# A transformer block on one core: the heads' sums loaded and inverted later, the feed-forward part started earlier

## The chip, the core and the metric

The kernel runs on one NeuronCore of a Trainium2 chip. Five instruction streams matter: TensorE (PE in the profile: matmuls and transposes), VectorE (DVE), ScalarE (ACT), GpSimd (POOL) and SyncE (SP, which issues nearly all DMAs). The metric is the device time of one launch in microseconds (us). Before the change the median of three runs is 856.14 us, with 854.97 the least and 856.69 the most.

## The reference

The input x has 4 sequences of 512 rows with 512 features. All is float32.

```python
x = x + attn(layernorm(x))
x = x + ffn(layernorm(x))

def attn(h):                                     # 32 heads of 16
    q, k, v = split(h @ w_attn + b_attn)
    s = q @ k.T / 16 + slope[head] * (key - row)  # ALiBi, causal
    return (softmax(s) @ v).reshape(...) @ w_proj + b_proj

def ffn(h):                                      # inner size 1376
    return (silu(h @ w_gate.T) * (h @ w_up.T)) @ w_down.T
```

layernorm has no weights; its eps is 1e-5.

## The kernel before, in words

**Slots.** The kernel writes its program through a heap of events. `at(t, fn, args)` puts a step at time t, in "slots"; `spread` lays a list of steps evenly between two times, `gemms` does that for matmul steps, and `later(dt, fn)` puts a step dt slots after the one that calls it. At the end the events are taken in order of time and each issues its instructions. A slot is no fixed time on the chip: the slots set the order only. In this kernel a slot of the attention phase is a little over one microsecond. PE keeps exactly this order, and so does SP's DMA queue (line 77, `Ordered`). Instructions that are wrapped in `pin` keep it too, among pinned ones of the same engine. The rest of DVE, ACT and POOL is ordered by a scheduler in the compiler.

**Precision.** Matmuls with weights are made of three products: each factor is split into a rounded high part (ACT, line 241 for weights) and a low part (DVE, line 242), and high*high, high*low and low*high are summed in a PSUM bank of 128x512 (eight banks in all).

**Attention.** There are 32 sub-units `su` of four heads, eight for each of the four sequences (b = 0 to 3), each 10 slots long. `pass_a` computes the scores from a stack of q and k (`st`), and DVE reads off their maxima (line 542: tile `bank` masked with `mask_t`, result read into M). A bank is free for the next scores only when DVE is through with it. `to_row` turns the maxima into rows of the stack (L571, and a DMA on POOL's queue). `pass_b` computes the scores again, ACT takes the exponential (L594, tile P), POOL masks the diagonal blocks (L596), and PE multiplies by v (bank<-P,v; starts at slot 10 su + 8.6). ACT copies the sums to `ue` (L616), and SP writes them to DRAM as `ud`. The stacks of a later sub-unit come back from DRAM by six DMAs `st<-qd` of 128 KB each. Where a tile is numbered, `st` has four buffers in turn.

**The heads' ends.** A unit u is two sub-units, eight heads; row 16 of each head's block in `ud` is the sum of its exponentials. The path is:

- `head_sums(u)`: SP loads the sums, lc<-ud, 16 KB. This can't start before both halves of `ud` have been written.
- `inverses(u)`: DVE takes the reciprocal, rc<-lc (line 641, pinned), and some slots later SP writes rd<-rc.
- `attn_heads(u)`: SP loads uc<-ud (256 KB) and rb<-rd, the inverse repeated over 16 rows (256 KB).
- `scaled_heads(u)`: POOL multiplies uc by rb (L662, pinned, so ahead of what the scheduler puts later on POOL), ACT (L665) and DVE (L666) split the product into `aT`.
- `proj_steps(b, t)`: matmuls of aT with w_proj; the input rows `xr` are loaded, POOL adds the bias (L434), DVE adds the bank (L438), and SP writes x1d<-xr to DRAM.

The projections of sequences 0, 1 and 2 are laid between the matmuls of the attention as filler for PE.

**Feed-forward.** `norm_steps` (from line 111) loads four tiles xt<-x1d, takes the statistics on DVE (L127, pinned, and L128), the root on POOL (L132, L134) and applies them on DVE (L144). `transposed` turns the tiles on PE (L88), and ACT and DVE split them into xnT. `ffn(b, times)` lays out, for each of eleven blocks of the inner size, the gate and up products (bank<-xnT,wf), ACT's Silu (L865), the product and its split (DVE L869 and L872, ACT L871), and the down product. `weights(t, kind, ...)` issues two loads (raw<-in_wgu or raw<-in_wd, 256 KB each) at slot t and their splits into `wf` six slots later. There are 17 such loads for the first sequence, and the weights then stay for the others.

**Buffers.** The tiles xt, raw, ue, uc, rb, xr and sg share nine buffers (tag "x"), in the order of their allocation; xnT, aT and hl share ten. SP has eight semaphore lanes, used in turn: a DMA on SP also waits until the one before it on its lane has landed.

The lines that the change touches: 47 (`ffn`), 647 (the delay of rd's write), 754 to 756 (times of `head_sums` and `inverses`), 757 to 761 (heads and projections of sequences 0 to 2), 765 (the projection of the last sequence), 831 to 834 (the weights' times) and 842 to 851 (the norm in `ffn`).

Of the kernel before, what the change touches and what calls it, by code (L numbers as in the profile page):

```python
# [24 lines left out]
NT = S // 128  # L25
NK = HID // 128
KM = 59
FAR = -30000.0
PRM = {
    'lv': 1,  # L30
    'lf': 0,
    'lg': 0,
    'P1': 4,
    'sv': [1, 2],
    'tn': 6,
    'vc': 1,
    'q3': 0.865,
# [6 lines left out]
    'pin': '',  # L44
    'wp': 84.0,
    'order': 's',
    'ffn': 311.954,
    'ffs': 8.623,
    'pj3': 346.0,
    'nb': 10.709,  # L50
# [10 lines left out]
def f(ap):  # L61
    return ap.bitcast(F32)
# [3 lines left out]
def block_kernel(ctx, tc, x, wqk, wv, bqk, bv, wp, bp, wgu, wgul, wd, cst, out):  # L66
    nc = tc.nc
    def pin(ins):
        return tc.keep_in_program_order(ins)
# [14 lines left out]
    def matmul(*args, **kw):  # L84
        tc.keep_in_program_order(nc.tensor.matmul(*args, **kw))  # L85
# [10 lines left out]
    def bank():  # L96
        return ps.tile([128, 512], F32, tag="bank", bufs=8, name="bank")
# [131 lines left out]
    def xnT_tiles(pl):  # L229
        return [pl.tile([128, 2, S], FR, tag="t4", bufs=PRM["t4"], name="xnT") for _ in range(NK)]  # L230
# [95 lines left out]
    def at(t, fn, *args):  # L326
        heapq.heappush(events, (max(t, clock["now"]), clock["n"], fn, args))
        clock["n"] += 1

    def later(dt, fn, *args):  # L330

        at(clock["now"] + dt, fn, *args)

    def spread(t0, t1, steps):
        for n, (fn, *args) in enumerate(steps):
            at(t0 + (n + 0.5) * (t1 - t0) / len(steps), fn, *args)

    def mm3_steps(get_p, pairs, done):

        todo = [(a, c) for (w, x2) in pairs for a, c in ((w(0), x2(0)), (w(0), x2(1)), (w(1), x2(0)))]  # L340
        box = {}

        def one(n):
            if n == 0:
                box["p"] = get_p()
            a, c = todo[n]
            matmul(box["p"], a(), c(), start=(n == 0), stop=(n == len(todo) - 1))
            if n == len(todo) - 1:
                done(box["p"])

        return [(one, n) for n in range(len(todo))]
# [64 lines left out]
    def proj_steps(b, t):  # L416
        c = slice(t * 128, t * 128 + 128)

        def w(k):
            return lambda h: (lambda: aTs[4 * b + k][:, h, c])  # L420

        def xx(k):
            return lambda h: (lambda: Wp[k // 2][:, h, k % 2, :])

        r0 = b * S + t * 128
        box = {}

        def start():
            box["xr"] = com.tile([128, HID], F32, tag="x", bufs=PRM["xb"], name="xr")
            sp.dma_start(box["xr"], x[r0 : r0 + 128, :])  # L430
            return bank()

        def add_bias():
            pin(pool.tensor_tensor(box["xr"], box["xr"], bp_t, ALU.add))  # L434

        def done(p):
            xr = box["xr"]
            dve.tensor_tensor(xr, p, xr, ALU.add)  # L438

            def send():  # L440
                sp.dma_start(x1d[r0 : r0 + 128, :], xr)
                made.add(("x1", b, t))

            later(4.5, send)

        steps = mm3_steps(start, [(w(k), xx(k)) for k in range(4)], done)
        return steps[:10] + [(add_bias,)] + steps[10:]
# [191 lines left out]
    def inverses(u):  # L639
        rc = com.tile([128, 32], F32, tag="rc", bufs=2, name="rc")  # L640
        pin(dve.reciprocal(rc, lcs[u]))

        def send():
            rds[u] = dr.tile([8, S], F32, tag="rd", bufs=16, name="rd")
            sp.dma_start(rds[u].rearrange("h (a q) -> (h a) q", a=16), rc)

        later(4.5 if u < 15 else 2.5, send)

    def attn_heads(u):

# [22 lines left out]
    def gemms(t0, t1, *items):  # L673
        spread(10.0 * t0, 10.0 * t1, [s for item in items for s in item])
# [50 lines left out]
    for su in range(NS):  # L725
        t0 = 10.0 * su
        t = t0 - 20.6
# [7 lines left out]
    for b in range(B):  # L735
        t = 8 * b
# [3 lines left out]
        if b + 1 < B:  # L740
            xT_next(b + 1, 10.0 * (t + PRM["xt"]) if b else 7.6)
            u = 4 * b + 4
# [9 lines left out]
                    t + 6.2, t + 8.2, qk_steps(u + 2, 0), qk_steps(u + 2, 1), v_steps(b + 1, 0), v_steps(b + 1, 1),  # L752
                )
    for u in range(4 * B):
        at(20.0 * u + 28.5, head_sums, u)
        at(20.0 * u + 33.0, inverses, u)
    for b, first, gap, p0, p1_ in ((0, 102.0, 5.0, 127.0, 148.0), (1, 182.0, 5.0, 207.0, 228.0), (2, 246.0, 6.0, 274.0, 298.0)):
        for k in range(4):
            at(first + gap * k, attn_heads, 4 * b + k)
            at(first + 8.0 + gap * k, scaled_heads, 4 * b + k)  # L760
        gemms(p0 / 10, p1_ / 10, *[proj_steps(b, t) for t in range(NT)])
    for u, t in ((12, 313.0), (13, 316.0), (14, 320.5), (15, 340.0)):
        at(t, attn_heads, u)
        at(t + 6.0, scaled_heads, u)
    gemms(PRM["pj3"] / 10, PRM["pj3"] / 10 + 4, *[proj_steps(3, t) for t in range(NT)])


    GU, DN = {}, {}
# [46 lines left out]
    def weights(t, kind, it, slot, wait=6.0):  # L815
        loads, rest = (gu_steps if kind == "gu" else dn_steps)(it, slot)
        for n, ((l, a), (r, c)) in enumerate(zip(loads, rest)):
            at(t + 0.5 * n * bool(wait), l, a)
            at(t + 0.5 * n * bool(wait) + wait, r, c)
# [5 lines left out]
    loads = []  # L825
# [2 lines left out]
        if it % 2 == 0:  # L828
            loads.append(("dn", it, len(loads)))

    for n, t in enumerate((297.0, 311.0, 305.0, 314.0, 328.0, 322.0)):
        weights(t, *loads[n])
    at(PRM["tl"], open_late)
    for n, t in enumerate((331.0, 345.0, 339.0, 348.0, 362.0, 356.0, 366.0, 379.0, 373.0, PRM["pj3"] + 36.0, PRM["pj3"] + 44.0)):
        weights(t, *loads[6 + n])

    def ffn(b, times):

        box = {}
        xs = []  # L840
        t0 = times[0]
        loads, rest = norm_steps(x1d, b, xs, (1,))
        spread(t0 - (23.0 if b else 24.0), t0 - (18.0 if b else 20.0), loads)
        spread(t0 - (15.5 if b else 18.0), t0 - (8.0 if b else 10.0), rest)

        def tp(k):
            if k == 0:
                box["xT"] = xnT_tiles(com)
            transposed(xs, box["xT"], [k])

        spread(t0 - 8.5, t0, [(tp, k) for k in range(NK)])

        def up_gate(it, t):
            m = min(128, INTER - it * 128)
            at_once = {}

            def w(g, k):
                return lambda h: (lambda: GU[it][:, h, g, k])

            def x2(k):  # L860
                return lambda h: (lambda: box["xT"][k][:, h, :])

            def gate(p):
                at_once["sg"] = sg = com.tile([128, S], F32, tag="x", bufs=PRM["xb"], name="sg")
                act.activation(sg[:m], p, AF.Silu)  # L865

            def up(p):
                sg = at_once["sg"]
                dve.tensor_tensor(sg[:m], sg[:m], p, ALU.mult)  # L869
                hl = com.tile([128, 2, S], FR, tag="t4", bufs=PRM["t4"], name="hl")  # L870
                act.copy(hl[:m, 0, :], sg[:m])  # L871
                dve.tensor_tensor(hl[:m, 1, :], sg[:m], f(hl[:m, 0, :]), ALU.subtract)  # L872
                box[it] = hl

            steps = []
            for g, done in enumerate((gate, up)):
                steps += mm3_steps(lambda: bank()[:m], [(w(g, k), x2(k)) for k in range(NK)], done)
            spread(t, t + PRM["ffs"] * 2 / 3, steps)

        def down(it, t):  # L880
            m = min(128, INTER - it * 128)

            def one(k, n, a, w):
                if it == 0 and k == 0 and n == 0:
                    box["accs"] = [bank() for _ in range(NT)]
                matmul(
                    box["accs"][k], box[it][:m, a, k * 128 : k * 128 + 128], DN[it][:m, w, :],
                    start=(it == 0 and n == 0), stop=(it == NIT - 1 and n == 2),
                )

            parts = ((0, 0), (1, 0), (0, 1))
            spread(t, t + PRM["ffs"] / 3, [(one, k, n, *p) for k in range(NT) for n, p in enumerate(parts)])

        def residual(t):
            r0 = b * S + t * 128
            box["xr", t] = xr = com.tile([128, HID], F32, tag="x", bufs=PRM["xb"], name="xr")
            sp.dma_start(xr, x1d[r0 : r0 + 128, :])

        def finish(t):
            r0 = b * S + t * 128  # L900
            xr = box["xr", t]
            dve.tensor_tensor(xr, box["accs"][t], xr, ALU.add)
            later(2.0, lambda: sp.dma_start(out[r0 : r0 + 128, :], xr))

        for it in range(NIT):
            up_gate(it, times[it])
            down(it, times[it] + PRM["ffs"] * 5 / 3)
        for t in range(NT):
            at(times[-1] + 9.5 + 0.5 * t, residual, t)
            at(times[-1] + 17.3, finish, t)  # L910

    for b in range(B):
        ffn(b, [PRM["ffn"] + PRM["ffs"] * (b * NIT + it) for it in range(NIT)])
# [61 lines left out]
```

## Time and profile before

| | |
|---|---|
| median of three runs | 856.14 us |
| profiled execution | 856.19 us, of which the span from first to last instruction is 854.3 |
| PE busy | 819.6 us |
| DVE, ACT, POOL busy | 472.0, 358.1, 274.4 us |
| mean granted TensorE clock | 0.992 |
| DMA | 98.98 MB, mean 116 GB/s |

The profile is of one execution. In its timeline a line gives the start in us, the time of the group, the engine, the line of the code and the operation, then output<-inputs by tile names, shapes, the number of instructions, and in brackets the idle time of that engine before and what ended it. The table of windows gives for each stretch of time its length, the busy time (and instructions) of PE, PE's weight loads, DVE, ACT and POOL, then the granted clock of TensorE (1.00 is full speed), the DMA engines' share and GB/s. The chain is the work that ended last, followed back: start, length, what. A wait for several semaphores is put down to the one that came last by the profile, so an engine named as releaser may itself have stood.

The attention phase with its filler lasts until about 475 us. From there to the end the feed-forward matmuls follow each other on PE.

### The profile page before, as it was taken

Reading aid. Unit: us, or ns where it says so; the run is one execution under the profiler, and the core shown is the slowest. Engines: PE = TensorE matmul, PEld = TensorE weight load, DVE = VectorE, ACT = ScalarE, POOL = GpSimd, SP = SyncE. Lnnn points to the kernel's source line nnn. Section 1 sums busy time; section 2 is a strip of 40 time slices with the busy share of each in tenths; the row PEclk is TensorE's granted clock in tenths of the full one; section 3 lists DMA queues with packets and bytes.
Section 4 is the critical chain, followed back from the end, with each engine's and each line's share of the span. In section 5 each row is a group of like instructions: output and inputs, shape, how many; then the busy total and the mean of one; then the engine's idle time right before and its main releaser. Section 6 shows DMA issues by size and latency. Waiting matters only on the chain.

```text
span 854.3 us, 13248 instructions
## 1 busy us (share of the span) xinstructions
PE 819.6 (96%) x4448; PEld 629.5 (74%) x4448; DVE 472.0 (55%) x1438; ACT 358.1 (42%) x678; POOL 274.4 (32%) x601
## 2 busy tenths in 40 slices
PE   6999999989999988999798999999999999999998
PEld 4867777756777766777476788878888888878886
DVE  7898888758885766667775554443114311431112
ACT  4646666665555664466557632221112111121111
POOL 5834565656544555546654211000000000000000
PEclk9999999999999989999999999999999999999999
DMA  6496987788956788777874534312000200010101
GB/s 216 130 191 114 177 188 124 167 153 215 233 129 92 161 156 189 144 167 149 173 181 138 186 112 148 112 39 82 18 25 25 74 25 13 25 63 13 37 1 50
DMA packets 56387, 98.98 MB, mean 116 GB/s; under 512 B 15384, under 2 KB 15640, under 8 KB 56144
## 3 DMA queue, kind: packets, MB, share of 16 engines
q1 hardware_dynamic: 51520, 94.73, 45.4%
q0 software_dynamic: 4800, 3.40, 3.1%
q8 instruction: 36, 0.59, 0.3%
q14 instruction: 31, 0.25, 0.1%
HBM read 65.05 MB, written 32.77 MB: 115 GB/s over the span
## 4 chain that ended last, share of the span: by engine, by line
PE 81%; DMA 10%; DVE 5%; issue 1%; ACT 1%; SPq 1%; POOL 0%; POOLq 0%; DVEq 0%; ACTq 0%
PE bank L85 79%; DMA st<-qd 4%; PE bank L88 2%; DMA lc<-ud 2%; DMA ud<-ue 2%; DVE bank L542 2%; DMA uc<-ud 2%; SPq L77 1%; ACT P L594 0%; DVE M L542 0%; DVE r L77 0%; DMA raw<-in_wv 0%; DVE st L127 0%; ACT wf L241 0%; DVE aT L666 0%
## 5 line engine op out<-in xcount | busy, mean ns | idle before, releaser
L542 DVE CUSTOM_DVE_ANT_0 bank<-bank,mask_t 128x512 f32<-128x512 f32 (+3 forms) x512 | 245.0, 507 | 88.0 <-PE bank L85 81.9
L85 PE MATMUL bank<-xnT,wf 128*128 128x512 f32 (+1 forms) x1056 | 257.7, 393 | 0.0
L85 PE MATMUL bank<-st 128*128 128x512 f32 (+3 forms) x896 | 239.1, 344 | 15.9 <-DVE M L542 9.6
L594 ACT ACTIVATE P<-bank 128x512 f32<-128x512 f32 (+1 forms) x352 | 191.4, 561 | 133.8 <-PE bank L85 127.9
L85 PEld LDWEIGHTS bank<-xnT,wf 128*128 128x128 f32 (+1 forms) x1056 | 195.4, 186 | 45.1 <-issue 0.2
L85 PEld LDWEIGHTS bank<-st 128*128 128x128 f32 x896 | 159.8, 193 | 44.7 <-DVE M L542 12.1
L596 POOL TENSOR_SCALAR_AFFINE_SELECT P<-P 128x128 f32<-128x128 f32 (+2 forms) x352 | 122.6, 353 | 146.8 <-ACT P L594 142.9
L85 PE MATMUL bank<-xnT,wqk_t 128*128 128x512 f32 x384 | 142.9, 406 | 0.0
L869 DVE TENSOR_TENSOR sg<-sg,bank 128x512 f32<-128x512 f32 (+1 forms) x44 | 30.2, 687 | 199.1 <-PE bank L85 199.0
L85 PE MATMUL bank<-wf,hl 128*128 128x512 f32 (+1 forms) x528 | 131.4, 393 | 0.0
L85 PEld LDWEIGHTS bank<-wf,hl 128*128 128x128 f32 (+1 forms) x528 | 98.9, 188 | 22.0
L865 ACT ACTIVATE sg<-bank 128x512 f32<-128x512 f32 (+1 forms) x44 | 26.3, 598 | 159.1 <-PE bank L85 155.8
L85 PEld LDWEIGHTS bank<-xnT,wqk_t 128*128 128x128 f32 x384 | 72.3, 190 | 23.8 <-issue 13.2
L85 PE MATMUL bank<-P,v 128*32 128x512 f32 (+3 forms) x1024 | 84.0, 443 | 1.3 <-POOL P L596 1.3
L871 ACT CAST hl<-sg 128x512 fp32r<-128x512 f32 (+1 forms) x44 | 27.3, 621 | 116.2 <-DVE sg L869 116.2
L85 PE MATMUL bank<-wrow_t,aT 128*128 128x512 f32 x192 | 71.9, 397 | 0.0
L542 DVE DVE_READ_ACCUMULATOR2_ANT M<- 128x1 f32 x512 | 71.7, 140 | 0.0
L132 POOL TENSOR_SCALAR ve<-mv 128x4 f32<-128x4 f32 x7 | 1.7, 237 | 211.3 <-DVE mv L128 211.3
L85 PE MATMUL bank<-wrow_t,xnT 128*128 128x512 f32 x192 | 65.0, 409 | 0.0
L85 PEld LDWEIGHTS bank<-P,v 128*32 128x32 f32 x1024 | 27.3, 110 | 42.3 <-issue 24.7
L872 DVE TENSOR_TENSOR hl<-sg,hl 128x512 fp32r<-128x512 f32 (+1 forms) x44 | 31.8, 723 | 24.3 <-ACT hl L871 24.1
L85 PEld LDWEIGHTS bank<-wrow_t,xnT 128*128 128x128 f32 x192 | 36.0, 192 | 8.6 <-issue 2.5
(78 smaller groups left out, 555.0 us busy)
## 6 DMA issues: line engine op xcount, KB each, us to landing
st<-qd SPq DMA_DIRECT2D x180, 128.0 KB
qd<-c SPq DMA_DIRECT2D x30, 512.0 KB
ud<-ue SPq DMA_DIRECT2D x32, 256.0 KB
raw<-in_wgu SPq DMA_DIRECT2D x20, 256.0 KB
xt<-in_x SPq DMA_DIRECT2D x16, 256.0 KB
uc<-ud SPq DMA_DIRECT2D x16, 256.0 KB
rb<-rd SPq DMA_DIRECT2D x16, 256.0 KB
xr<-in_x SPq DMA_DIRECT2D x16, 256.0 KB
```

What stands on the lines that cost most here:

```text
L77: return lambda *args, **kw: tc.keep_in_program_order(fn(*args, **kw))
L85: tc.keep_in_program_order(nc.tensor.matmul(*args, **kw))
L88: tc.keep_in_program_order(nc.tensor.transpose(*args))
L132: pin(pool.tensor_scalar(ve, box["mv"][:, :, 1], EPS, None, ALU.add))
L542: dve.tensor_tensor_reduce(s, s, mask_t[:, S - w : S], -1.0, 3.0e38, ALU.add, ALU.min, m[:, n : n + 1])
L594: act.activation(pt, p[:, :w], AF.Exp)
L596: pool.affine_select(d, d, pattern=[[0, len(heads)], [1, 128]], compare_op=ALU.is_ge, fill=0.0, base=0, channel_multiplier=-1)
L865: act.activation(sg[:m], p, AF.Silu)
L869: dve.tensor_tensor(sg[:m], sg[:m], p, ALU.mult)
L871: act.copy(hl[:m, 0, :], sg[:m])
L872: dve.tensor_tensor(hl[:m, 1, :], sg[:m], f(hl[:m, 0, :]), ALU.subtract)
```

## The change

- The sums of a unit u are loaded at slot 20u + 35 and inverted at 20u + 44 (before: 28.5 and 33). Unit 11 has 30.5 and 36.5; units 14 and 15 keep the old times. The write of the inverse comes 2.5 slots after the inverse, not 4.5, from unit 11 on (before: for unit 15 only).
- The heads of sequence 2 are fetched four slots later (250 to 268), and its projection is laid over slots 280 to 302, not 274 to 298. The last sequence's projection takes 33 slots, not 40.
- The feed-forward part begins at slot 305, not 311.954. Its first norm is moved further ahead: loads from 278 (before 288), statistics and the rest from 283 (294), transposes from 292.5 to 302 (303.5 to 312).
- The weights' loads come earlier: the first two pairs of gate and up weights by 31 and 33 slots, the others by 4 to 8.

The instructions are the same but for two more loads of an activation table on ACT; what changes is the order.

```diff
-    'ffn': 311.954,
+    'ffn': 305.0,
...
-        later(4.5 if u < 15 else 2.5, send)
+        later(4.5 if u < 11 else 2.5, send)
...
     for u in range(4 * B):
-        at(20.0 * u + 28.5, head_sums, u)
-        at(20.0 * u + 33.0, inverses, u)
-    for b, first, gap, p0, p1_ in ((0, 102.0, 5.0, 127.0, 148.0), (1, 182.0, 5.0, 207.0, 228.0), (2, 246.0, 6.0, 274.0, 298.0)):
+        sums, inverse = (28.5, 33.0) if u >= 14 else ((30.5, 36.5) if u == 11 else (35.0, 44.0))
+        at(20.0 * u + sums, head_sums, u)
+        at(20.0 * u + inverse, inverses, u)
+    for b, first, gap, p0, p1_ in ((0, 102.0, 5.0, 127.0, 148.0), (1, 182.0, 5.0, 207.0, 228.0), (2, 250.0, 6.0, 280.0, 302.0)):
         for k in range(4):
             at(first + gap * k, attn_heads, 4 * b + k)
-            at(first + 8.0 + gap * k, scaled_heads, 4 * b + k)
+            at(first + (8.0 if b < 2 or k < 3 else 9.0) + gap * k, scaled_heads, 4 * b + k)
         gemms(p0 / 10, p1_ / 10, *[proj_steps(b, t) for t in range(NT)])
...
-    gemms(PRM["pj3"] / 10, PRM["pj3"] / 10 + 4, *[proj_steps(3, t) for t in range(NT)])
+    gemms(PRM["pj3"] / 10, PRM["pj3"] / 10 + 3.3, *[proj_steps(3, t) for t in range(NT)])
...
-    for n, t in enumerate((297.0, 311.0, 305.0, 314.0, 328.0, 322.0)):
+    for n, t in enumerate((266.0, 303.0, 272.0, 307.0, 321.0, 315.0)):
         weights(t, *loads[n])
     at(PRM["tl"], open_late)
-    for n, t in enumerate((331.0, 345.0, 339.0, 348.0, 362.0, 356.0, 366.0, 379.0, 373.0, PRM["pj3"] + 36.0, PRM["pj3"] + 44.0)):
+    for n, t in enumerate((326.0, 338.0, 332.0, 341.0, 355.0, 349.0, 359.0, 372.0, 366.0, PRM["pj3"] + 30.0, PRM["pj3"] + 40.0)):
         weights(t, *loads[6 + n])
...
         loads, rest = norm_steps(x1d, b, xs, (1,))
-        spread(t0 - (23.0 if b else 24.0), t0 - (18.0 if b else 20.0), loads)
-        spread(t0 - (15.5 if b else 18.0), t0 - (8.0 if b else 10.0), rest)
+        spread(t0 - (23.0 if b else 27.0), t0 - (18.0 if b else 23.0), loads)
+        spread(t0 - (15.5 if b else 22.0), t0 - (8.0 if b else 13.0), rest)
...
-        spread(t0 - 8.5, t0, [(tp, k) for k in range(NK)])
+        spread(t0 - (8.5 if b else 12.5), t0 - (0.0 if b else 3.0), [(tp, k) for k in range(NK)])
```

## The prediction, made before the changed kernel ran

> **What bounds the kernel now.** I read the summary of engines first, then the chain that ended last, then TensorE's idle gaps in the timeline, and last who caused the two longest.
>
> ```profile
> PE 819.6 (96%) x4448; PEld 629.5 (74%) x4448; DVE 472.0 (55%) x1438; ACT 358.1 (42%) x678; POOL 274.4 (32%) x601
> PE 81%; DMA 10%; DVE 5%; issue 1%; ACT 1%; SPq 1%; POOL 0%; POOLq 0%; DVEq 0%; ACTq 0%
> ```
>
> TensorE (PE) is busy 96% of 854.3 us. It leaves 34.7 us idle, 7.9 at the start and 3.8 at the end. So matmuls set the time, and a change of order can only win back gaps and the slow clock that follows some of them. The gaps that matter here, from the timeline (in brackets the idle time before, and its releaser):
>
> ```profile
> 193.16 1.44 PE L85 MATMUL bank<-st 128*128 128x256 f32 x3 [4.58 <-DVE M L542]
> 306.72 1.44 PE L85 MATMUL bank<-st 128*128 128x256 f32 x3 [3.28 <-DVE M L542]
> 327.86 0.47 PE L85 MATMUL bank<-st 128*128 128x512 f32 x1 [2.41 <-DMA st<-qd]
> 411.96 0.97 PE L85 MATMUL bank<-st 128*128 128x512 f32 x3 [1.85 <-DMA st<-qd]
> 425.65 0.47 PE L85 MATMUL bank<-st 128*128 128x512 f32 x1 [1.63 <-DMA st<-qd]
> 454.72 1.75 PE L88 MATMUL bank<-ident,xt 128*128 128x128 f32 x4 [1.31 <-DVE xt L144]
> ```
>
> Three smaller ones are 1.49 us at 415.21 and 1.18 at 452.09 (both behind DVE's maxima), and 0.75 + 0.52 at 474.00 and 475.14 (behind POOL's P). From 475 to 850 there is none. The first two are named for DVE, but DVE was itself standing, at the reciprocal of the heads' sums:
>
> ```profile
> 192.10 0.35 DVE L641 RECIPROCAL rc<-lc 128x32 f32<-128x32 f32 x1 [5.37 <-DMA st<-qd]
> 305.67 0.35 DVE L641 RECIPROCAL rc<-lc 128x32 f32<-128x32 f32 x1 [4.09 <-DMA lc<-ud]
> ```
>
> The chain says why: the sums' load (lc) stands on SP until the unit's second half (ud) has been written, and then takes 9 to 10 us beside other transfers.
>
> ```profile
> 173.00 9.27 DMA ud<-ue
> 182.34 9.68 DMA lc<-ud
> 192.10 0.35 DVE rc L641
> ```
>
> Before 305.67 the chain holds 8.61 (ud) and 8.97 (lc). The other 14 reciprocals waited little. Each lost stretch is longer than its gap, for the granted clock (the third column from the right) falls:
>
> ```profile
> 190.00:200.00 10.00, 6.84 (x35) 4.57 (x35) 6.87 (x25) 2.98 (x5) 4.05 (x8) 0.83 0.59 173
> 300.00:310.00 10.00, 6.72 (x29) 5.50 (x27) 5.80 (x20) 5.35 (x11) 4.38 (x12) 0.78 0.85 113
> 310.00:320.00 10.00, 10.00 (x64) 6.46 (x65) 7.62 (x29) 6.23 (x14) 6.09 (x13) 0.87 0.82 189
> 450.00:460.00 10.00, 7.18 (x49) 5.22 (x52) 7.26 (x22) 7.74 (x16) 5.80 (x14) 0.83 0.46 160
> ```
>
> A clock of 0.83 over 10 us is 1.7 us lost; 0.78 and 0.87 are 2.2 + 1.3 = 3.5, of which half a microsecond fell on a PE that was idle anyway: 3.0.
>
> **The change, part by part.** The sum is made against the profiled execution, 856.19 us (span 854.3 and 1.9 around it), 0.05 above the median. There are as many matmuls, VectorE, POOL and DMA instructions as before; ACT has two more.
>
> *A. Sums and inverses later (14 units; 35/44 slots for 28.5/33).* At every unit lc (16 KB) now stands on SP behind a ud that had time to land, and rc comes 7.5 us or more behind lc's issue. SP stood 51.4 us at ud (17 times); most of that goes, so what is queued behind lc on SP (st, uc, rb loads) is issued earlier. On DVE, behind rc stand the maxima that empty PE's banks, and PE waits for those.
>
> First place, 183 to 215 us: 4.58 + 1.7 = 6.3 us to win. What is late next: POOL's product uc*rb, in order, ahead of the masks of P.
>
> ```profile
> 191.52 1.26 POOL L662 TENSOR_TENSOR uc<-uc,rb 128x512 f32<-128x512 f32 x1 [3.90 <-DMA st<-qd]
> 206.65 1.29 POOL L662 TENSOR_TENSOR uc<-uc,rb 128x512 f32<-128x512 f32 x1 [1.87 <-DMA rb<-rd]
> ```
>
> The first waits in truth for rb of head group 1 (issued 176.99, 14.38 us to land, 191.38), which the change does not hasten; two masks behind it end at about 193.3, and with everything else ready PE waits some 1.3 us there. The second's rb is issued some 2 us earlier than 197.19; PE runs 5 us earlier, so it loses some 1.7. The stacks for the next sub-unit (st, last issue 202.63, 8.06 to land) come 3 us earlier, PE more: 1.0. I take 6.3 - 1.3 - 1.7 - 1.0 = 2.3, between 0 (all given back) and 6.3 (PE's eight banks bridge it).
>
> Second place, 285 to 330: 3.28 + 3.0 = 6.3, and 2.41 at 327.86, 8.7 in all. The st load that releases PE at 327.86 was issued at 319.41, behind rb of group 7; the SP order puts it some 3.8 us earlier. If that load still ends the wait, 3.8 are won, and PE stands 8.7 - 3.8 = 4.9 us somewhere before it, which by the two rows above costs clock again, 1.7 to 3.0. I take 3.8 - 2.3 = 1.5, between -1.5 (the load only 1.5 earlier) and 8.7. The reciprocal itself: lc issued at about 307, an estimate of 314 for its landing, DVE there at 312; this wait of 2 us lies inside the 4.9.
>
> *B. Heads of batch 2 four slots later, proj2 at 280 to 302 for 274 to 298.* The eight 256 KB loads (uc, rb) pass behind one st group on SP, so the 1.85 at 411.96 goes. But proj2's matmuls were the filler in 410 to 425; six slots go without, so PE reaches the stack of 425.65 some 6 us earlier while its loads, issued from 417.64 to 419.54 (5.54 to land), gain 1 to 3: a wait of about 4.0 for 1.63. With half a chance of a lost clock window (0.9): 1.85 - 2.4 - 0.9 = -1.5. Bounds: +5.0 (1.85, 1.49 and 1.63 all go) and -6.
>
> *C. First weights and first norm ahead (two pairs of raw loads 31 and 33 slots, xt loads 10, statistics and transposes 11).* Four 256 KB weight loads and four 256 KB xt loads go past SP's st loads of 400 to 440, 2.6 to 4.5 us each by their rows after 434 (xt 2.99, 2.90, 3.89, 4.51; raw 2.93 to 3.10). Their splits (4 each on ACT and DVE, 0.64 and 0.6 us) lie beside matmuls with ACT at 50 to 75% and DVE at 55 to 85%; uncovered, they would cost up to 5 us. What they may delay is in B's bound and in the slower rival. The gain is at 449 to 476: the norm and its transposes are no longer the last thing there, and FFN matmuls, from slot 305, fill PE: 1.18 + 1.31 + 0.75 + 0.52 + 1.7 of clock = 5.5 at most. ACT was at 8.78 of 10 us in 460 to 470 and keeps Exp and Silu work mixed, so I take 4.0, between 0 and 5.5. The two extra activation-table loads (1.28 us each in the row of Silu) are covered by ACT's idle quarter; uncovered, 2.6.
>
> *D. proj3 in 33 slots for 40, later weight loads 5 to 8 slots ahead.* After 475 PE has no gap, and the loads keep their 15 slots ahead of use: 0, cover being PE's own 375 us. Bounds -1 and +0.5.
>
> Sum: 2.3 + 1.5 - 1.5 + 4.0 = 6.3; 856.19 - 6.3 = 849.9.
>
> The row on the clock: it halved after idle stretches of 4.58 and 3.28 us, and at 456 after stretches of 1.18 and 1.31 only; 2.41 at 327 cost none. The Trainium skill ("TensorE: Matmul & The Clock Gate", section "What's actually happening") says the array falls to half clock after at least one idle window of about 3.4 us. By that, waits cut into pieces as mine are would cost no clock, and the sum would be 2.3 + 0.9 better, 846.7; the trace's drop at 456 contradicts it, and I keep the charge.
>
> **Rivals.**
> *R1, the waits go altogether.* Once DVE and SP stand no more, PE's banks bridge POOL's waits. For it: POOL is 55 to 75% busy in these stretches; the other reciprocals' units show no gap. Against: rb takes 9 to 14 us there, DMA share 0.83 to 0.98. First place 6.3, second 6.3, third 0, fourth 5.5: 18.1, so 838.1; halfway from the forecast, 844.
>
> *R2, the transfers bound these stretches.* lc merely stops being the one named: uc, rb and st end as before, rc waits at slot 44 too. The change then does not do what it says. First and second 0, third -1.5, fourth 2.0: 855.7. For it: DMA share 0.98 in 200 to 210. Against: SP's 51.4 us of standing at ud are real and go.
>
> *R3, slower.* At 410 to 440 the moved weight and xt loads stand ahead of st on SP. DVE's norm statistics, which it takes in order, come 11 slots earlier, about 434 to 435 on the old clock, while the last two xt would land at an estimated 432 to 437; DVE stands up to 3, PE behind it, st is late by 4 to 6, and the clock falls twice (3.4). Price up to 12.4; it decides once this place loses more than the 7.8 won elsewhere. 856.19 - 7.8 + 12.4 = 860.8. For it: DMA share 1.06 in 420 to 430. Against: raw and xt tiles are issued only as buffers come free.
>
> **How the numbers follow.** Forecast (842 to 854) 0.54, R1 0.19, R2 0.12, R3 0.15. Runs of this kernel differ by 0.2% (1.7 us), so faster means under 854.4. Faster: nearly all of the forecast, R1 and a quarter of R2, 0.73; same 0.11; slower 0.16. Leaving out the far half of R1 and of R3: 840 to 858.5. The likeliest case alone: 845 to 854.
>
> **What would show it.** A: both long gaps at DVE's maxima and both idle times ahead of the reciprocal gone, the chain without lc; SP's wait for ud well under 51; in their place POOL waits at uc for rb, and gaps of 1 to 2 us at masks or st near 190, 203 and 322. B: no gap near 409, one of 3 to 5 before the stack near 420. C: the clock at 1.00 where FFN begins, transposes amid proj2. D: no gap in the last 370 us. I am wrong if PE's gaps from 180 to 330 total under 5 us (R1) or as much as before (R2), or if DVE's statistics show idle time ended by xt loads (R3).

## The result: 1% slower, and the profile after

The changed kernel takes 863.98 us in the median of four runs (862.60 to 865.35), beside 855.68 for the kernel before on the same chip. The ratio is 1.0096, with a 95% interval from 1.0076 to 1.0116. The prediction was 849.9, with 858.5 as its upper end: the sign was wrong and the range did not hold the time. The profiled execution took 865.35 us, the longest of the four, with a span of 863.5, 9.2 more than the span before.

The summary of engines, for the kernel after:

```profile
PE 824.4 (95%) x4448; PEld 629.8 (73%) x4448; DVE 469.8 (54%) x1438; ACT 361.0 (42%) x680; POOL 276.0 (32%) x601
```

PE's idle time ahead of its instructions, from the timeline of the kernel after:

```profile
193.99 1.08 PE L85 MATMUL bank<-P,v 128*32 128x384 f32 x4 [1.51 <-POOL P L596]
209.82 1.74 PE L85 MATMUL bank<-P,v 128*32 128x384 f32 x4 [3.62 <-POOL P L596]
...
312.96 0.76 PE L85 MATMUL bank<-st 128*128 128x512 f32 x1 [3.00 <-DMA qd<-c]
328.44 1.08 PE L85 MATMUL bank<-P,v 128*32 128x384 f32 x4 [1.70 <-POOL P L596]
...
416.03 1.23 PE L85 MATMUL bank<-st 128*128 128x512 f32 x3 [2.55 <-DMA st<-in_cst]
432.68 1.19 PE L85 MATMUL bank<-st 128*128 128x512 f32 x2 [6.73 <-DMA st<-qd]
437.26 0.37 PE L88 MATMUL bank<-ident,M 128*32 128x128 f32 x1 [1.10 <-DVE M L542]
456.49 1.70 PE L88 MATMUL bank<-ident,xt 128*128 128x128 f32 x4 [0.63 <-DVE xt L144]
```

The windows of the kernel after in which the granted clock (third column from the right) fell, and the one at 450 in which it no longer does:

```profile
210.00:220.00 10.00, 9.89 (x49) 6.24 (x48) 5.59 (x15) 4.50 (x10) 5.16 (x11) 0.83 1.00 221
310.00:320.00 10.00, 7.04 (x31) 4.81 (x32) 3.71 (x12) 3.30 (x7) 4.23 (x8) 0.66 0.68 170
420.00:430.00 10.00, 5.63 (x36) 3.19 (x34) 6.71 (x25) 4.94 (x11) 4.42 (x10) 0.92 0.97 155
430.00:440.00 10.00, 6.22 (x28) 4.07 (x29) 4.32 (x13) 4.18 (x8) 3.52 (x7) 0.50 0.93 199
440.00:450.00 10.00, 10.00 (x56) 7.59 (x55) 8.40 (x32) 4.97 (x9) 4.02 (x10) 0.89 0.76 181
450.00:460.00 10.00, 8.98 (x53) 6.34 (x52) 8.70 (x29) 4.94 (x10) 5.34 (x11) 1.00 0.26 84
```

The waits that the change aimed at are gone: none of the 16 reciprocals finds DVE idle ahead of it, lc is no longer in the chain, and SP's waits for ud no longer stand among its twelve largest (51.4 us before). But the time went elsewhere. I compare the two executions by the starts of ACT's copies of ue (L616), one for each sub-unit, which stand at the same point of the program in both. They begin 0.56 us apart, which other runs of the same instructions do too. After that:

| place | what it cost more than before, us | from |
|---|---|---|
| 183 to 230 | +2.0 | ue of sub-units 10 and 13: +0.46, +2.50 |
| 298 to 335 | +1.2 | ue of sub-units 18 and 20: +2.64, +3.82 |
| 405 to 445 | +10 | gaps 2.55 + 0.45 + 6.73 + 1.10 for 1.85 + 1.49 + 1.63, so 5.9; the clock 6.9 us below full, some 2.7 of it while PE was idle, so 4.2 |
| 449 to 476 | -4.8 | 0.63 for 1.18 + 1.31 + 0.75 + 0.52 + 1.7 of clock |
| 480 to the end | 0 | PE full in both |

With the 0.6 at the start this makes 9.0 of the 9.2.

**In the first two places POOL took over from DVE.** From POOL's timeline in the kernel after:

```profile
208.26 1.26 POOL L662 TENSOR_TENSOR uc<-uc,rb 128x512 f32<-128x512 f32 x1 [6.86 <-DMA rb<-rd]
```

POOL stands 6.86 us for rb, where it stood 1.87 before, and the masks of P behind it on POOL hold PE for 3.62. This rb was issued at 196.10, 1.1 us earlier than before, and landed at 208.12, 1.6 us later (times of the two profiles as they are, without the 0.56 us of the start).

**In the third place a stack came late.** PE's 6.73 us end with `st<-qd`, the stack of sub-unit 30. Its loads read what `qd<-c` wrote to DRAM just before, so they can't be issued until that has landed. SP's queue there, before the change:

```profile
405.04 0.60 SPq L77 DMA_DIRECT2D uc<-ud  x1
406.18 0.58 SPq L77 DMA_DIRECT2D rb<-rd  x1
...
409.67 0.39 SPq L77 DMA_DIRECT2D qd<-c  x1
...
417.28 2.69 SPq L77 DMA_DIRECT2D st<-qd  x6
```

and after it:

```profile
404.97 0.60 SPq L77 DMA_DIRECT2D uc<-ud  x1
405.62 0.58 SPq L77 DMA_DIRECT2D rb<-rd  x1
...
407.47 0.43 SPq L77 DMA_DIRECT2D raw<-in_wgu  x1
410.43 0.37 SPq L77 DMA_DIRECT2D qd<-c  x1
410.85 0.47 SPq L77 DMA_DIRECT2D raw<-in_wgu  x1
411.41 0.60 SPq L77 DMA_DIRECT2D uc<-ud  x1
412.06 0.58 SPq L77 DMA_DIRECT2D rb<-rd  x1
420.71 2.66 SPq L77 DMA_DIRECT2D st<-qd  x6
```

Two moved weight loads and two pairs of heads' loads now stand around qd, where one pair of heads' loads stood before. qd's write takes 10.22 us, not 7.55, and the last stack load takes 9.25, not 5.54; the stack is complete at 432.2, not 425.1. In both kernels qd was issued 0.03 us after DVE had made its c, and the first st 0.06 us after qd had landed: neither their order on SP nor a buffer held them, the transfers themselves took longer. At the same time ACT stands, in order, at the split of a moved weight:

```profile
432.77 0.62 ACT L241 CAST wf<-raw 128x512 fp32r<-128x512 f32 x1 [7.30 <-DMA raw<-in_wgu]
```

Both waits end within 0.1 us of each other, so the profile alone leaves open which of them held PE.

### The profile page after: what moved, and what is told of

It reads as the page before. It is cut to its first block, busy times and chain, and to the rows that moved or that the text cites. A ratio compares the mean times of both kernels' runs of the same rounds, so it can differ in the third digit from the quotient of the medians.

```text
span 863.5 us, 13225 instructions
## 1 busy us (share of the span) xinstructions
PE 824.4 (95%) x4448; PEld 629.8 (73%) x4448; DVE 469.8 (54%) x1438; ACT 361.0 (42%) x680; POOL 276.0 (32%) x601
## 4 chain that ended last, share of the span: by engine, by line
PE 86%; DMA 9%; DVE 3%; issue 1%; POOL 0%; ACT 0%; SPq 0%; POOLq 0%; ACTq 0%
PE bank L85 83%; DMA st<-qd 4%; PE bank L88 2%; DMA raw<-in_wgu 2%; DMA rb<-rd 1%; DVE bank L542 1%; DMA qd<-c 1%; DMA xr<-in_x 0%; DVE r L77 0%; DMA xt<-in_x 0%; SPq L77 0%; ACT P L594 0%; DVE xt L144 0%; DVE M L542 0%; POOL r L77 0%
## 5 line engine op out<-in xcount | busy, mean ns | idle before, releaser
L85 PE MATMUL bank<-P,v 128*32 128x512 f32 (+3 forms) x1024 | 87.4, 446 | 6.8 <-POOL P L596 6.8
L85 PEld LDWEIGHTS bank<-wrow_t,aT 128*128 128x128 f32 x192 | 37.1, 196 | 7.6 <-issue 1.2
```

## The experiments

Ratios are to the kernel before, run on the same chip, with 95% intervals; they need not equal the ratio of the two medians. All are within 2% of 1; I call a difference clear where its interval leaves out 1. All edits are to the kernel before ("before") or the changed one ("after").

**1. The later sums alone.** Before, with the new times of `head_sums` and `inverses` and the new delay of rd's write:

```diff
-        at(20.0 * u + 28.5, head_sums, u)
-        at(20.0 * u + 33.0, inverses, u)
+        sums, inverse = (28.5, 33.0) if u >= 14 else ((30.5, 36.5) if u == 11 else (35.0, 44.0))
+        at(20.0 * u + sums, head_sums, u)
+        at(20.0 * u + inverse, inverses, u)
```

> The kernel before with only the later sums and inverses (and the shorter delay of rd's write). The changed kernel lost 2.0 us from 183 to 215 and 1.2 from 298 to 335 against the old times of ue, after both waits at the reciprocal had gone. Theory A (the later sums cost time by themselves, POOL's product waiting for rb in their place): 858 to 860 us, POOL waits at uc<-uc,rb of 25 to 31 us in all, gaps at P,v of 3 to 4 us near 209. The prediction's step A: 852 us. Rival (the losses there come from other parts of the change): 850 to 854.

Measured: 859.02 us, 1.0032 (1.0017 to 1.0047), as theory A has it. POOL's and PE's timelines in this run show the same exchange as in the full change:

```profile
207.41 1.26 POOL L662 TENSOR_TENSOR uc<-uc,rb 128x512 f32<-128x512 f32 x1 [6.81 <-DMA qd<-c]
```

```profile
208.97 1.08 PE L85 MATMUL bank<-P,v 128*32 128x384 f32 x4 [3.61 <-POOL P L596]
```

(POOL's releaser is named qd, but rb landed at 207.27.) The later sums by themselves cost 0.3%, where step A had them win 3.8 us.

**2. The early weights back.** After, with the first two pairs of gate and up weights at 290 and 298:

```diff
-    for n, t in enumerate((266.0, 303.0, 272.0, 307.0, 321.0, 315.0)):
+    for n, t in enumerate((290.0, 303.0, 298.0, 307.0, 321.0, 315.0)):
```

> The changed kernel with the first two pairs of gate and up weights loaded at slots 290 and 298 (15 slots and 7 ahead of the feed-forward start) in place of 266 and 272. Theory T (ACT stands 7.30 us at the split of a weight whose load landed at 432.75, and PE behind it 6.73, with the clock halved until 442): the gap at 432 and the low clock go, 8 to 12 us, so 852 to 856 us. Rival U (the missing six slots of proj2 matmuls leave PE without work until the stack lands): 861 to 865, with a gap of 3 us or more before a stack at 420 to 435 still there.

Measured: 856.59 us, 1.0008 (0.9986 to 1.0030). Moving these four loads and their splits back wins 0.9%, as much as the whole loss of the change. A gap of 4.58 us before the stack stays, at 423.81 (in a profiled execution of 853.22 us): rival U's mark is there too, at a time just above theory T's 852 to 856.

**3. Heads and projection of sequence 2 back.** After, with `(2, 246.0, 6.0, 274.0, 298.0)` for `(2, 250.0, 6.0, 280.0, 302.0)` and 8 slots for the last product, not 9.

> The changed kernel with the heads of sequence 2 at 246 and its projection at 274 to 298 again. Rival U (missing filler): 854 to 857. Theory T in its plain form (the weight's split on ACT): 860 to 864, ACT idle at L241 for 5 us or more. A third reading (the weight's buffer was late only because the heads of sequence 2 were, since raw takes the buffers that uc and rb leave): ACT's wait shrinks below 2 us and the time is 854 to 858 with the weights left where the change put them.

Measured: 858.74 us, 1.0038 (1.0012 to 1.0064); ACT waits 1.5 us for raw, and the gaps in 405 to 445 are 1.37, 2.31 and 0.90. The third reading has the wait of ACT right and its 854 to 858 just too low. With sequence 2 back 0.6% of the loss is gone, though the early weights stay.

**4. The early weights alone.** Before, with 266 and 272 for 297 and 305.

> The kernel before with only the first two pairs of weights moved to slots 266 and 272. Theory T in its plain form: a wait of ACT at L241 of 5 us or more, and 862 to 868 us. Third reading (the late heads' buffers are needed for the harm): ACT's wait under 2 us, 854 to 858. Rival U: 855 to 857, nothing new in 405 to 445.

Measured: 860.08 us, 1.0042 (1.0021 to 1.0062), with 2.8 us of waiting for raw on ACT; the gap before the stack near 430 is 0.65 us, that at 415, 3.15. The weights hurt alone too, by half of what they do in the full change. The third reading had 854 to 858 and a wait under 2 us, plain T 862 to 868, rival U 855 to 857: all three miss.

**5. What is left without the three parts.** After, with the sums, sequence 2 and the first weights as in experiments 1 to 3 undone.

> The changed kernel without three of its parts: sums and inverses at the old slots, heads and projection of sequence 2 at the old slots, first two weight pairs at 290 and 298. What is left is the feed-forward part and its norm seven to eleven slots earlier and the last projection in 33 slots. If the parts add up (later sums +2.7 us as measured alone, weights about +7.4, and these rest), 863.9 - 2.7 - 7.4 gives about 853.5, and the gaps at 452 and 454 and the low clock at 456 are gone. Rival (the earlier feed-forward part gains nothing): 856 to 857.

Measured: 855.33 us, 0.9998 (0.9979 to 1.0016). At the place of the norm (447 to 459 here) this run has 2.4 us of gaps and a full clock, where the kernel before has 3.8 and 1.7 of clock; in the total it can't be told from no gain.

**6. Heads' loads earlier.** As experiment 1, and:

```diff
-            at(first + gap * k, attn_heads, 4 * b + k)
+            at(first - (0.0, 5.0, 4.0)[b] + gap * k, attn_heads, 4 * b + k)
```

> The kernel before with the later sums and, beside them, the loads of uc and rb of sequences 1 and 2 issued 5 and 4 slots ahead of where they were, POOL's products staying in place. Theory A2 (after the reciprocal's wait is gone, POOL's product, which stands for rb in order and holds the masks of P, is what PE waits for): the gaps at P,v near 193, 209 and 329 go, and the time is 851 to 855. Rival (the transfers are the limit, earlier rb loads only delay st and ud): 858 to 861, with longer gaps ended by st<-qd.

Measured: 854.29 us, 0.9976 (0.9952 to 1.0000), an interval that just reaches 1. Between sub-units 18 and 20 this run is 7.6 us quicker than before, while experiment 1 is 1.1 slower there. The gaps at 193 and 210 stay (1.88 and 4.00 us): the products that stand there are those of sequence 0, whose loads I had left alone.

**7. The splits later, the loads where they are.** After, with the splits of the first two weight pairs 18 slots behind their loads, not 6:

```diff
-        weights(t, *loads[n])
+        weights(t, *loads[n], wait=18.0 if n in (0, 2) else 6.0)
```

> The changed kernel with the loads of the first two weight pairs where the change put them, but their splits on ACT and DVE 18 slots after the load, not 6. Theory T (ACT stands at the split in order): 853 to 858, ACT waits for raw under 1 us. Rival (the loads themselves, ahead on SP and holding buffers of tag x, delay lc, xt, ud and st): 861 to 866, the gap before the stack near 430 stays at 4 us or more.

Measured: 862.48 us, 1.0087 (1.0064 to 1.0110). ACT stands for raw no longer, and yet, in PE's timeline of this run:

```profile
430.70 1.19 PE L85 MATMUL bank<-st 128*128 128x512 f32 x2 [7.63 <-DMA ud<-ue]
```

The stack's last load landed at 430.2 in this run. Theory T falls for the changed kernel: the split on ACT only ended at the same moment. With experiment 2, the loads themselves do the harm.

**8. Early weights back and heads' loads earlier.** After, with the edit of experiment 2 and loads 5 slots earlier for sequences 1 and 2.

> The changed kernel with the first weights at 290 and 298 and the loads of uc and rb of sequences 1 and 2 issued 5 slots earlier. If theory A2 and theory T both hold, the gaps near 193, 209 and 322 and the one at 432 go: 846 to 851, faster than the kernel before. If the transfers are the limit: 856 to 860.

Measured: 853.19 us, 0.9976 (0.9959 to 0.9993). Place two is won, place one is not, as in experiment 6; 846 to 851 was too much.

**9. All heads' loads earlier.** As experiment 6, with `(5.0, 5.0, 4.0)[b]`.

> The kernel before with the later sums, and the loads of uc and rb of sequences 0, 1 and 2 issued 5, 5 and 4 slots earlier. The run with sequences 1 and 2 alone won 7.5 us between sub-units 18 and 20 against the run with the sums alone, and nothing near 209 us, where it is the products of sequence 0 that stand on POOL: its rb of unit 3 was issued at 196.60 and landed 12.47 us later. Theory A2 (POOL's product standing for rb is what replaced the reciprocal's wait): the gap at P,v near 209 (4.0 us, and 2.5 of clock) goes here too, 849 to 852. Rival (the place near 209 is bound by the amount of transfers): the gap moves to a stack, 854 to 857.

Measured: 848.28 us, 0.9903 (0.9874 to 0.9933), faster than before. POOL's timeline in this run, around the place where it stood 6.8 us:

```profile
195.87 1.28 POOL L662 TENSOR_TENSOR uc<-uc,rb 128x512 f32<-128x512 f32 x1
...
199.67 1.30 POOL L662 TENSOR_TENSOR uc<-uc,rb 128x512 f32<-128x512 f32 x1
```

No product of sequences 0 to 2 waits, and PE has no gap near 209. Theory A2 is shown: what took the place of the reciprocal's wait was POOL, standing for rb. Before the stack at 406.73 PE stands 7.63 us in this run.

**10. Combined.** After, with early weights and sequence 2 back and the loads of experiment 9.

> The changed kernel with the first weights at 290 and 298, the heads and the projection of sequence 2 at the old slots, and the loads of uc and rb of sequences 0, 1 and 2 issued 5, 5 and 4 slots earlier. If later sums, earlier head loads and an earlier feed-forward part each keep what they won: 846 to 850, faster than both kernels. If the earlier feed-forward part gains nothing: as the run with the sums and all head loads early, within 2 us.

Measured: 847.76 us, 0.9907 (0.9878 to 0.9935). The earlier feed-forward part adds nothing to experiment 9 that can be measured. The stack near 407 finds PE idle for 7.80 us, as in experiment 9 (7.63).

**11. Only the second early weight pair back,** from 272 to 298.

> The changed kernel with only the second of the two early weight pairs put back, from 272 to 298; the first stays at 266. Theory T2 (the weights' transfers lie between the write of q and k of unit 15 and the reads of its stack, and lengthen both; the late split on ACT was shown to be no cause): the first pair delays the write (10.22 us in place of 7.46), the second the reads (9.25 in place of 8.8), so about two thirds of the 7.5 us stay: 859 to 862, gap before the stack near 428 of 4 to 7 us. Rival (the second pair is the harmful one, since SP stands 3.4 us at its buffer): 855 to 858.

Measured: 860.21 us, 1.0045 (1.0022 to 1.0069), gap 6.31. About half of the 0.9% stays. Theory T2 gave the time; its split in detail was off, for qd's write took 8.7 us here (10.2 with both pairs).

**12. Heads of sequence 2 earlier, projection not.** After, with the loads of sequence 2 at 246 to 264.

> The changed kernel with the loads of uc and rb of sequence 2 four slots earlier, at 246 to 264 as before the change, all else (its projection at 280 to 302, the early weights) as changed. Theory T2 (it is the crowd of transfers around 405 to 430, head loads and weights together, that delays the stack): 856 to 860. Rival U (the missing six slots of projection as filler): 862 to 865.

Measured: 866.63 us, 1.0096 (1.0059 to 1.0133), above both ranges. The six executions spread from 860.30 to 868.67 us; the profiled one took 860.30. Nothing is won: the wait is now in two pieces, 5.73 at 413.59 and 3.32 at 428.43.

**13. Projection of sequence 2 back, heads not.** After, with 274 to 298 for 280 to 302.

> The changed kernel with only the projection of sequence 2 laid over slots 274 to 298 again; its heads' loads stay at 250 to 268 and the early weights stay. If the missing filler is half of the loss at 425 to 445: 857 to 861 us, ratio 1.002 to 1.006, the gap before the stack near 432 below 3 us. If the heads' loads (crowding the transfers) are: 863 to 866, the gap stays.

Measured: 867.67 us, 1.0129 (1.0093 to 1.0166), above both ranges. PE's timeline in this run:

```profile
437.33 0.80 PE L85 MATMUL bank<-wrow_t,aT 128*128 128x512 f32 x1 [8.72 <-ACT aT L665]
```

The filler is there, but it waits itself, for an aT whose rb landed at 431.72 and whose ACT step stood behind the weight's split until 436.04. So neither half of sequence 2's move explains the loss alone. Put back together (experiment 3) they take 0.6% off, each alone takes nothing: here the filler fills only if its own inputs come ahead of the crowd.

**14. The best found.** After, with the first weights at 290 and 298 and the loads of uc and rb of sequences 0 and 1 five slots earlier; sequence 2 as changed:

```diff
-            at(first + gap * k, attn_heads, 4 * b + k)
+            at(first - (5.0, 5.0, 0.0)[b] + gap * k, attn_heads, 4 * b + k)
...
-    for n, t in enumerate((266.0, 303.0, 272.0, 307.0, 321.0, 315.0)):
+    for n, t in enumerate((290.0, 303.0, 298.0, 307.0, 321.0, 315.0)):
```

> The changed kernel with the first weights at 290 and 298 and the loads of uc and rb of sequences 0 and 1 five slots earlier; heads and projection of sequence 2 stay as changed. If the move of sequence 2 is no loss without the early weights: 844 to 848, gaps near 405 and 420 of 2 to 4 us each and no halved clock there. If it is a loss: 849 to 853.

Measured: 844.85 us (844.18 to 845.25), 0.9864 (0.9833 to 0.9895). What is left of PE's gaps in its timeline:

```profile
194.25 0.47 PE L85 MATMUL bank<-st 128*128 128x512 f32 x1 [2.62 <-DMA lc<-ud]
...
399.86 0.47 PE L85 MATMUL bank<-st 128*128 128x512 f32 x1 [1.39 <-DMA st<-in_cst]
414.21 1.19 PE L85 MATMUL bank<-st 128*128 128x512 f32 x2 [5.62 <-DMA xt<-x1d]
```

Two more, at 304.48 and 435.88, are 0.60 and 0.63. The time is as expected. The gap of 5.62 and a clock of 0.50 from 415 to 420 are not; there is still something to win before that stack.

**15. The combined kernel with sequence 2's loads at the old slots,** 246 to 264, projection at 274 to 298.

> The combined kernel that took 847.8 us, with the heads of sequence 2 loaded at 246 to 264, not four slots earlier, and its projection at 274 to 298. Its stack near 407 found TensorE idle for 7.8 us behind these loads: if they are what delays it, the gap falls to 3 to 5 us and the time to 843 to 846; if TensorE is simply early there, the time stays at 847 to 849.

Measured: 846.50 us, 0.9887 (0.9854 to 0.9919). The gap near 404 is 3.72 us, not 7.80, and the time half a microsecond above the 843 to 846 that went with it. The intervals of this, of experiment 10 and of experiment 14 overlap.

**16. Heads' loads earlier without the later sums.** Before, with `(5.0, 5.0, 0.0)[b]` alone.

> The kernel before with only the loads of uc and rb of sequences 0 and 1 five slots earlier; sums, inverses and all else as before. If the reciprocal's wait is a cost of its own (step A): DVE still stands about 4 to 5 us at rc near 190 and 305, and the time stays at 853 to 857. If the earlier loads thin the transfers so that lc lands in time by itself: 846 to 850, no wait at rc, and the later sums are of no use.

Measured: 850.72 us, 0.9936 (0.9908 to 0.9963). DVE's timeline at the two reciprocals:

```profile
194.22 0.35 DVE L641 RECIPROCAL rc<-lc 128x32 f32<-128x32 f32 x1 [5.90 <-DMA st<-qd]
304.91 0.35 DVE L641 RECIPROCAL rc<-lc 128x32 f32<-128x32 f32 x1 [1.63 <-DMA lc<-ud]
```

The time lies between the two ranges, and each expectation holds at one place: at the first the reciprocal's wait is as before and PE stands 5.09 us; at the second the thinner traffic alone does it (PE's gap is 0.82). Later sums and earlier loads were worth +0.3% and -0.6% alone. Together they are worth about -1.0%, more than the sum of the two (experiment 9, where sequence 2's loads are four slots earlier as well).

## Why the prediction was wrong

**Step A, mis-sized and of the wrong sign.** The place, the cause and the successor were named rightly: the reciprocal's wait went, and POOL's product for rb came in its stead. The failing terms are "issued some 2 us earlier ... it loses some 1.7" and "the SP order puts it some 3.8 us earlier": both let a transfer land earlier by as much as it is issued earlier. Measured, rb of unit 3 was issued 1.1 us earlier and landed 1.6 later (12.02 us, not 9.30), POOL stood 6.86, and PE lost 3.62 and 1.7 of clock at that point alone. The st load of the second place, issued at 319.41 before, was issued at 320.21, with the kernel 2.6 us behind at that place, and took 10.91 us, not 7.99. Without SP's stand the transfers around that rb came out closer together (thirteen on SP, from uc to the last st, in 8.1 us, not 11.2), and they took longer: the six st loads behind that rb 11.2 to 13.1 us, not 8.1 to 10.2. The two places gave -2.0 and -1.2 us, for +2.3 and +1.5.

**Step B, outside its bounds.** It had -1.5 between -6 and +5, and its place measured -10, with what step C's loads did there. The stack's loads were to "gain 1 to 3" with "5.54 to land". They came 7.1 us later, for I had followed their order on SP and not what they read: they start when qd has landed. The kernel was 3.8 us behind already at sub-unit 25; qd was issued only 0.8 later than before, but its write took 2.7 longer and the last read 3.7 longer. The failing term is these two durations, taken as they were before the change. The wait of "about 4.0" is near the 4.58 of experiment 2, where the weights are back. What the sum lacked is the harm of step C's loads to the stack, which step C named only as "in B's bound". Experiments 2 and 3 show that most of the loss goes when either the weights or sequence 2 are put back.

**Step C, right where it looked for a gain, wrong where it looked for a cost.** The gain at 449 to 476 was 4.8 for 4.0, with the clock at 1.00; with the other three parts undone, in experiment 5, a gain shows at that place but none in the total. The cost of the moved loads was put down as their splits' time and as landing times "by their rows after 434", 2.6 to 4.5 us. In the crowd at 407 to 428 they took 6.0 to 10.7, and they were the dear part of the change: 0.9% (experiment 2). PE has no gap where the extra table loads stand (474 to 496).

**Step D** was right: nothing changed after 480.

**The rivals.** R3 named the place (410 to 440) and nearly the price (12.4 for 10, 860.8 us in all) and had 0.15. Of its mechanism the late stack and the clock were right. DVE's statistics did not stand for xt; DVE's one long idle time there, 6.71 us, ended with ACT's split. R2's thought that rb, uc and st would end as before was nearer than the forecast at the first two places; its 855.7 was not, for the third. By the prediction's own sign R2 was met there: PE's gaps in 180 to 330 sum to 9.8 us (1.51 + 3.62 + 3.00 + 1.70), after 10.3 (4.58 + 3.28 + 2.41). But its condition, that rc waits at slot 44 too, was not: no reciprocal finds DVE idle. R1 was the opposite of what happened; experiment 9 shows the state it described, which takes earlier loads to reach.

**The clock.** It was halved behind 6.73 us of idle PE, behind 3.62 and behind 3.00. It was not behind 2.55 at 416. It was in experiments 9 and 15 near 305, behind 1.97 and 1.75. The Trainium skill ("TensorE: Matmul & The Clock Gate", section "What's actually happening") ties the fall to at least one idle window of about 3.4 us. These runs show it after shorter waits, so the charge of the prediction stood. It was too small: step B had 0.9 us, and in 405 to 445 the clock cost 4.2 beyond the idle time.

**What the traces tell apart, and what stays open.** The loss before the stack near 425 has two legs, and over the runs each goes with another part of the change. Where the heads' loads of sequences 0 and 1 are at their places, qd's write took 8.5 to 10.7 us in the seven kernels with one or both early weight pairs and 7.3 to 7.6 in the four without (the kernel before and experiments 1, 2 and 5); in the seven others, without early weights, it took 6.3 to 9.2. The last read took 8.5 to 10.6 us in the six kernels with the heads of sequence 2 at 250 to 268, early weights or not, and 5.4 to 6.1 in all twelve others. The runs that differ by one edit say the same: the weights alone take the write from 7.55 to 10.27 (experiment 4), and the heads' loads put back take the read from 9.25 to 5.90 (experiment 12). So the early weights lengthen the write and the later heads' loads the read. What each leg is worth in time stays open: experiment 12, with its short read, is no quicker, since the stack ahead of it came late. The remaining 5.62 us before that stack in the best kernel were not taken apart either.

## What to carry to other kernels

Taking a wait out of a queue need not bring what is behind it earlier by as much: here the loads came out together, and each took longer. So follow every load that something waits for to its landing in the crowded stretch, with durations from that stretch, and through DRAM to the write that it reads. Move early what an in-order engine will stand for (here the heads' loads of sequences 0 and 1, 0.6% alone), and late what nobody waits for yet (here the first weights, 0.9%); and a filler helps only when its own inputs don't come through the same crowd.

## What the runs showed of the hardware that was not expected

The same 256 KB weight load took very different times. Before the change the first four took 2.9 to 3.4 us (issued at 446.31 to 452.48; DMA share 0.54 and 0.46 in these windows). In the kernel after, the same four, issued at 407.47 to 427.38, took 10.7, 10.4, 9.3 and 6.0 us (DMA share 0.95, 0.80 and 0.97). The load of rb of unit 11, also 256 KB, took 15.25 us there (412.06 to 427.31). The core as a whole moved no more meanwhile: 182, 191 and 155 GB/s in these windows, beside 182 and 160 in those before.
